# Three early blocks instead of two ahead of a mixture-of-experts pass, and a pass that begins with only its first kind of block made ready

## The chip, the cores and the metric

The kernel runs on one core of one Trainium2 chip. The metric is the device time of one launch in microseconds (us); before the change the median of three runs was 2474.57 us (2471.67 to 2475.16). A row of the profile names the engine: PE is TensorE's matmul and PEld its weight load, DVE is VectorE, ACT is ScalarE, POOL is GpSimd, SP is SyncE, which here only issues transfers. L1563 is line 1563 of the kernel before.

## The reference

The input is `x`, 64 graphs of 256 nodes with 256 features (16,384 tokens), and an integer adjacency matrix per graph. Two layers follow each other:

```
x = x + graph_attention(layernorm(x), adj)
x = x + mamba2(layernorm(x))
x = x + relational_conv(layernorm(x), adj)
x = x + moe_ffn(layernorm(x))          # 8 experts, the best one per token

# moe_ffn, for each token t:
idx  = argmax(softmax(t @ gate_w + gate_b))
y    = relu(t @ w1[idx] + b1[idx]) @ w2[idx] + b2[idx]    # 256 -> 1024 -> 256
y    = y * probability(idx)                               # zero beyond an expert's capacity
y    = nan_to_num(y)
```

An expert takes at most 2,560 tokens. Only the last line, the mixture of experts (MoE), and the point where the rest hands over to it, are touched by the change, apart from one small store at the very start.

## The kernel before

**Pass 1** does everything up to the choice of the expert. It goes through the tokens in 32 groups of 512 rows. Its instructions are not written in the order in which they run: each step is recorded with a duration, the tiles that it reads and writes, and a rank, and a planner (`Plan`, a list scheduler) lays them out once, at build time. The rank of a step of group g is `PACE * g` plus an entry of the table `DUE`; the steps that come behind all groups take theirs from the table `LATE`, in the order in which they are recorded. A tile has a name (a "home") with a fixed number of buffers; a step that needs a home is laid out after the steps that use its previous tenant. The program order on each engine's queue is what the planner gave; the engines wait for each other by semaphores.

Each group stores its rows into `x3d` in memory and, for every token, a slot of four numbers (token number, weight, mean, scale) into `slots`, which is sorted by expert. `out` already has the rows at that point; the MoE part overwrites them.

**Early blocks.** An expert's tokens are worked on in blocks of 512 slots. When 28 of the 32 groups are routed, `list_first` picks the first `NEARLY` blocks that are already full, and `first_block` records their whole computation with the planner, so that it can be laid between the last groups' steps. Such a block fetches its slots and the expert's weights (SP), gathers its 512 rows from `x3d` by four indirect DMAs of 128 rows (L409, POOL), normalises them (L415, DVE), turns them (L1367 on PE, with copies on ACT), multiplies by `w1` (the L744 row `ps<-eT,gate` or its twin for block 0; ReLU at L1379 on ACT), by `w2` (L1388), adds the bias (L1394), scales (L1396, ACT), replaces non-finite values (`guarded`, L420 to L424), adds the residual (L1402) and scatters four times 128 rows into `out` (L427, POOL). The block has no memory of its own: it lives in homes of pass 1. Block 0 has `xT`, `xn`, `xnT` and four buffers of `x`, block 1 has `adji`, `wh`, `eT` and three of `dm`; each has one of the two buffers of `gate` (for `w1`) and of `xh` (for `w2`).

`list_blocks` then lists the remaining work: full blocks of 512 ("wholes"), and of each expert's rest, at most one block of 256 ("halves") and blocks of 128 ("quarters").

**Pass 2** (`second_pass`) has three loops, quarters, halves, wholes, in this order; each is a nest of `tc.If`, one per block, so its trip count is known only at run time. The trace shows 4 quarters, 1 half and 18 wholes. Each kind has a class `Blocks` with three buffers for slots and rows and two for weights (quarters with odd numbers use the wholes' second weight buffers). The body, `experts(i)`, first fetches the weights of block i+1 (`fetch_weights`, L1511 to L1520: `w1`, `b1`, `w2`, `b2`, all on SP's queue) and the slots of block i+2 (`fetch_slots`, L1502), gathers the rows of block i+2, normalises block i+1, then does its own multiplication by `w1` (32 matmuls at L1563, ReLU at L1567), by `w2` (16 matmuls per 128 rows, L1573), turns block i+1 in the middle (`turned`: L1545 on PE, L1548 on ACT), and finishes its rows (L1578, L1579, L420 to L424, L1586, L427).

So whatever block 0 of a loop needs has to be made ready before the loop. The kernel before does this for all three kinds ahead of the first loop, step by step in the order of its code: six slot fetches (blocks 0 and 1 of each kind), six gathers (14 indirect DMAs, since a whole takes four, a half two and a quarter one), three weight fetches, three times normalise and turn. Then comes a test, `general` (L1612 to L1617: two DVE instructions, a tiny matmul and a copy), whose outcome decides after pass 2 whether the inputs need a second, general form of the kernel. Pass 2's tiles lie in the memory that pass 1's homes had; a write waits for the last use of the home under it.

**The very start.** Before pass 1, the weights are prepared. One result, `b1` in a transposed form, is written to memory (`b1d`, L591) from SP's queue; SP then issues the loads of the first groups (L805 for `adj`, L803 for `x`).

Of the kernel before, what the change touches and what calls it, by code (L numbers as in the profile page):

```python
# [9 lines left out]
F32 = mybir.dt.float32  # L10
# [4 lines left out]
ALU = mybir.AluOpType  # L15
AX = mybir.AxisListType
# [3 lines left out]
P = 128  # L20
# [39 lines left out]
    1921, 332, 270, 332, 389, 145, 449, 139, 514, 497, 334, 177, 408, 502, 1660, 1834, 1843, 1988,  # L60
    2202, 2247, 2273, 2186, 2179, 1985, 1853, 1933, 1944, 2220, 1882, 2133, 1815, 2009, 2179,
    2095, 1789, 1828, 563, 1802, 1733, -146, 109, 1792, 2073, 414, 1763, 1943, 143, 509, 2344,
    2010, 508, 2033, 2085, 250, 423, 2196, 2256, 716, 2018, 1585, 411, 176,
]


# [221 lines left out]
def gnn_mamba_rgcn_moe(ctx: ExitStack, tc: tile.TileContext, a: dict, out: bass.AP):  # L288
# [12 lines left out]
    nc = tc.nc  # L301
    x, adj = a["x"], a["adj"]
    B, N, D = x.shape
    assert N == 256 and D == 256 and B % 2 == 0
    T = B * N
    NG = B // 2
# [26 lines left out]
    b1d = dram.tile([E, P, NFT], F32, name="b1d")  # L333
# [6 lines left out]
    for blk in (0, 2):  # L340
        nc.gpsimd.affine_select(
            out=tri[:, blk, :], in_=tri[:, blk, :], compare_op=ALU.is_ge, fill=0.0,
# [3 lines left out]
    upper, ones_pp = tri[:, 0, :], tri[:, 1, :]  # L346
# [29 lines left out]
    work = const.tile([1, 3, 2, NBLK], I32, name="work")  # L376


    NEARLY = 2
    early = const.tile([1, 2, NEARLY], I32, name="early")  # L380
    taken = const.tile([P, E], F32, name="taken")
    num_i = const.tile([P, NBLK], I32, name="num_i")
# [5 lines left out]
    tested = const.tile([P, NG], F32, name="tested")  # L388
    general = const.tile([1, 1], I32, name="general")
# [42 lines left out]
    def first_pass(form, pass1):  # L432
# [28 lines left out]
        for q in range(2):  # L461
            nc.scalar.dma_start(
                out=dch[q * 64 : (q + 1) * 64, :], in_=dskip[q : q + 1, :].broadcast_to([64, NCT])
# [50 lines left out]
        with tc.tile_pool(name="prep" + form, bufs=1) as prep, tc.tile_pool(  # L514
            name="prep_ps" + form, bufs=2, space=PSUM
# [8 lines left out]
                out=gq0[:, :, 0:E], in_=a["L1_ffn_gate_w"].rearrange("(k p) e -> p k e", p=P)  # L524
# [10 lines left out]
            for vec, dst in (("L0_ffn_b_lin", blin), ("L1_gnn_bias", brel)):  # L535
                col = prep.tile([P, 2], F32, tag="col", name="col", bufs=2)
                nc.sync.dma_start(out=col, in_=a[vec].rearrange("(k p) -> p k", p=P))
                ps = prep_ps.tile([P, 512], F32, tag="ps0", name="ps")
                for k in range(2):
                    nc.tensor.matmul(  # L540
                        ps[:, : E + 1], lhsT=col[:, k : k + 1].to_broadcast([P, P]),
                        rhs=gq[:, k, : E + 1],
                        start=(k == 0), stop=(k == 1),
# [4 lines left out]
            for i in range(2):  # L548
                nc.sync.dma_start(
                    out=av[:, i, :],  # L550
                    in_=a["L0_gnn_a"][i * D : (i + 1) * D, :].rearrange("d o -> o d").broadcast_to([P, D]),
# [17 lines left out]
            for k in range(2):  # L569
                ps = prep_ps.tile([P, DI], F32, tag="ps0", name="ps")  # L570
# [5 lines left out]
            for c in range(NCT):  # L576
                ps = prep_ps.tile([P, DG], F32, tag="ps0", name="ps")
                for k in range(2):
                    nc.tensor.matmul(
                        ps, lhsT=woT[:, k, c * P : (c + 1) * P], rhs=wl[:, k, :],  # L580
                        start=(k == 0), stop=(k == 1),
# [5 lines left out]
            ps = prep_ps.tile([P, E * NFT], F32, tag="ps0", name="ps")  # L587
            nc.tensor.transpose(ps, b1r, ident[: E * NFT, : E * NFT])
            b1t = prep.tile([P, E, NFT], F32, name="b1t")
            nc.vector.tensor_copy(b1t.rearrange("p e k -> p (e k)"), ps)  # L590
            nc.sync.dma_start(out=b1d.rearrange("e p k -> p e k"), in_=b1t)  # L591


        xv = x.rearrange("b (h p) d -> p (b h) d", p=P)
# [24 lines left out]
        def counted(s, tot):  # L619

            ps, seen_ = s.psum(), s.fixed(seen)
            s.step(PE, 0.1, lambda: nc.tensor.matmul(
                ps()[:, :E], lhsT=tri_b[:, 1, :], rhs=seen, start=True, stop=True), [seen_], [ps])
            s.step(DVE, 0.08, lambda: nc.vector.tensor_copy(tot(), ps()[:, :E]), [ps], [tot])
# [5 lines left out]
        def walk(s, we, wb, past, n, ends, gap, limit, to):  # L630

            v = nc.vector
            s.step(DVE, 0.07, lambda: v.memset(we(), 0.0), [], [we])
            for e in range(E - 1):
                def passed(e=e):
                    v.tensor_scalar(past(), num[:, :n], ends()[:, e : e + 1], None, ALU.is_ge)
                    v.tensor_add(we(), we(), past())
                    v.scalar_tensor_tensor(wb(), past(), gap()[:, e : e + 1], wb(), ALU.mult, ALU.add)  # L640

                s.step(DVE, 0.4, passed, [ends, gap], [we, wb, past])

            def listed():
                v.tensor_scalar(wb(), wb(), float(limit - 1), None, ALU.min)
                v.tensor_copy(to[:, 0, :n], we()[0:1, :])
                v.tensor_copy(to[:, 1, :n], wb()[0:1, :])

            s.step(DVE, 0.25, listed, [we, wb], [s.fixed(to)])

        def list_first(s):
# [3 lines left out]
            tot, full, ends, gap = (s.tile(n + "_", [P, E]) for n in ("tot", "full", "ends", "gap"))  # L655
            we, wb, past = (s.tile(n + "_", [P, NEARLY]) for n in ("we", "wb", "past"))
            counted(s, tot)
# [14 lines left out]
            def took():  # L672
                v.tensor_scalar(tot(), ends(), float(NEARLY), None, ALU.min)
                v.tensor_copy(taken[:, 0:1], tot()[:, 0:1])
                v.tensor_sub(taken[:, 1:], tot()[:, 1:], tot()[:, : E - 1])
                v.tensor_scalar(gap(), full(), -1.0, float(NB), ALU.mult, ALU.add)
                v.tensor_copy(wb(), num[:, :NEARLY])

            s.step(DVE, 0.5, took, [ends, full], [tot, gap, wb, s.fixed(taken)])
            walk(s, we, wb, past, NEARLY, ends, gap, NBLK, early)  # L680

# [606 lines left out]
        def first_block(s, b, stored, source):  # L1288
# [5 lines left out]

            w1, w2 = s.tile("gate", [P, NCT, 512], bufs=2), s.tile("xh", [P, NCT, 512], bufs=2)
            side = s.tile("hide", [P, 4, N], BF16, bufs=3)
            if b == 0:
                xg, xn, xnT = s.tile("xT", [P, 2, 512]), s.tile("xn", [P, 4, D]), s.tile("xnT", [P, 2, 512])
                hid = [s.tile("x", [P, 4, DQ], bufs=5) for _ in range(4)]
            else:  # L1300
                xg, xn, xnT = s.tile("adji", [P, 4, N], I32), s.tile("wh", [P, 4, WX]), s.tile("eT", [P, 2, 512])
                hid = [s.tile("dm", [P, 2, 2, N + P], bufs=NCT) for _ in range(3)]
            each = NFT // len(hid) + (NFT % len(hid) > 0)

            def hidden(f):
                t = hid[f // each]()
                t = t.rearrange("p a b c -> p (a b c)") if b else t.rearrange("p a b -> p (a b)")
                return t[:, (f % each) * 512 : (f % each + 1) * 512]


# [51 lines left out]
            for k in range(2):  # L1362
                ps = s.psum()
# [10 lines left out]
            for f in range(NFT):  # L1374
                ps = s.psum()
# [6 lines left out]
            for j in range(4):  # L1382
                ps = s.psum()
# [39 lines left out]
        if form == "fast":  # L1423
# [15 lines left out]
            list_blocks(plan)  # L1439
            for b in range(NEARLY):  # L1440
                first_block(plan, b, rows_early, x3d[0 : GEARLY * 4 * P])
# [21 lines left out]
    def second_pass(form, pass2):  # L1463
        et = pass2.enter_context(tc.tile_pool(name="et" + form, reuse_waits="tile", bufs=2))
        es = pass2.enter_context(tc.tile_pool(name="es" + form, reuse_waits="tile", bufs=4))
        eps = pass2.enter_context(tc.tile_pool(name="eps" + form, reuse_waits="tile", bufs=8, space=PSUM))
# [124 lines left out]
        quarters = Blocks(2, wholes)  # L1591
# [6 lines left out]
        ]  # L1598
        three = (quarters, halves, wholes)
        for blocks in three:  # L1600
            for i in range(2):
                blocks.fetch_slots(i)
        for blocks in three:
            for i in range(2):
                blocks.gather(i, nc.gpsimd)
        for blocks in three:
            blocks.fetch_weights(0)
        for blocks in three:
            blocks.turned(blocks.norm(0), 0)
        if form == "fast":  # L1610
            other = es.tile([P, NG], F32, tag="yv", name="other")
            nc.vector.tensor_scalar(other, tested, float(N) + 1.0, None, ALU.is_gt)  # L1612
            others = es.tile([P, 1], F32, tag="others", name="others", bufs=1)
            nc.vector.tensor_reduce(others, other, AX.X, ALU.max)
            ps = eps.tile([P, 512], F32, tag="ps", name="ps")
            nc.tensor.matmul(ps[:, 0:1], lhsT=ones_pp, rhs=others, start=True, stop=True)
            nc.vector.tensor_copy(general, ps[0:1, 0:1])  # L1617
        for blocks in three:
            with ExitStack() as nest:  # L1619
                for i in range(blocks.most):  # L1620
                    nest.enter_context(tc.If(listed[blocks.kind] > i))
                    blocks.experts(i)


    for form in ("fast", "slow"):
        with ExitStack() as here:
            if form == "slow":
                again = nc.values_load(
                    general[0:1, 0:1], min_val=0, max_val=P,
                    skip_runtime_bounds_check_because="a count of partitions",  # L1630
                )
                here.enter_context(tc.If(again > 0))
            with ExitStack() as pass1:
                first_pass(form, pass1)
            with ExitStack() as pass2:
                second_pass(form, pass2)
# [34 lines left out]
```

## Time and profile before

The profile is of one execution, 37 us longer than the median of the runs.

| | us |
|---|---|
| median of the runs (lowest, highest) | 2474.57 (2471.67, 2475.16) |
| the profiled execution's own time | 2511.58 |
| its span, first to last instruction | 2509.9 |
| mean granted TensorE clock in it | 0.979 |
| PE busy (share of the span) | 2360.5 (94%) |
| DVE busy | 1917.8 (76%) |
| ACT busy | 1644.8 (66%) |
| POOL busy | 817.3 (33%) |

The page cuts the span into 40 slices of 62.7 us and gives each engine's busy share in each as a digit of tenths (9 is 90% or more), and the granted clock likewise. A row of the timeline has a start, a duration, the engine and line, the tiles (output, then inputs), the count of instructions run together, and in brackets the idle time before it with what ended it. A row of the windows view has, for a stretch of time, its length, each engine's busy time with a count, the granted clock, the busy share of the DMA engines and GB/s.

### The profile page before, as it was taken

The page shows a single profiled execution, that of the slowest core. Times are in us where ns is not written, and L with a number is a line of the kernel's source. Part 1 is how long each engine was busy: PE and PEld are TensorE (multiplying, and loading weights), DVE is VectorE, ACT ScalarE, POOL GpSimd, SP SyncE. Part 2 cuts the span into 40 slices and gives each one's busy share as a digit, 9 for nine tenths or more (in the row PEclk, how much of TensorE's full clock was granted, in tenths as well). Part 3 has the DMA queues.
Part 4 walks back from the last instruction along what each step waited for, and adds up shares of the span by engine and source line. Part 5 has one row for each costly group of instructions (what it writes and reads, how often), then busy time and mean ns, then how long its engine had stood idle before and what let it go on. Part 6 is the DMA issues. An engine that isn't in the chain of part 4 may idle for free.

```text
span 2509.9 us, 35018 instructions
## 1 busy us (share of the span) xinstructions
PE 2360.5 (94%) x11451; PEld 1645.5 (66%) x11451; DVE 1917.8 (76%) x4825; ACT 1644.8 (66%) x3720; POOL 817.3 (33%) x762
## 2 busy tenths in 40 slices
PE   5999999999999999999999999999986899999996
PEld 3667676767667666766766676676655666666664
DVE  4899899999989998998999999999863343344333
ACT  2878888878888887888888888887522233222331
POOL 1132424333342433334243333423423223222231
PEclk8999999999999999999999999999997999999998
DMA  3212222322222322222232222223337433333332
GB/s 115 44 23 62 54 71 65 71 54 54 62 54 71 68 68 54 54 62 54 70 71 65 54 54 62 57 59 55 105 96 244 135 128 112 124 108 112 124 113 65
DMA packets 173527, 198.93 MB, mean 79 GB/s; under 512 B 25448, under 2 KB 157870, under 8 KB 173312
## 3 DMA queue, kind: packets, MB, share of 16 engines
q1 hardware_dynamic: 124816, 135.70, 16.8%
q0 software_dynamic: 46816, 58.88, 12.8%
q8 instruction: 98, 1.61, 0.3%
q10 hardware_dynamic: 1680, 1.79, 0.3%
q14 instruction: 117, 0.96, 0.1%
HBM read 112.47 MB, written 45.45 MB: 63 GB/s over the span
## 4 chain that ended last, share of the span: by engine, by line
issue 31%; DVE 30%; PE 18%; POOL 10%; ACT 7%; DMA 3%; POOLq 0%; another core or an unknown queue 0%; SPq 0%; ACTq 0%; DVEq 0%
PE ps L744 12%; DVE y L963 8%; POOL xg L409 3%; POOL out_dram L427 3%; DVE gate L946 3%; POOL rs L752 3%; PE ps L1095 2%; DVE gate L1108 2%; DVE st L760 2%; DVE xh L1105 2%; DVE dm L1088 2%; DMA xg<-x3d,place 1%; DVE ev L857 1%; DVE bm L973 1%; DVE ev L859 1%
## 5 line engine op out<-in xcount | busy, mean ns | idle before, releaser
L744 PE MATMUL ps<-xnT,win 128*128 128x512 f32 x1152 | 544.5, 602 | 4.0 <-ACT xnT L786 4.0
L963 DVE SCALAR_TENSOR_TENSOR y<-ps,cw,y 128x510 f32<-128x510 f32 (+2 forms) x480 | 350.6, 737 | 6.5 <-ACT y L956 5.4
L1030 ACT ACTIVATE dm<-ps,cs 128x256 f32<-128x256 f32 (+1 forms) x1024 | 335.6, 480 | 24.2 <-PE ps L744 23.6
L752 POOL TENSOR_TENSOR rs<-ve,mhalf 128x4 f32<-128x4 f32 x96 | 149.0, 1552 | 570.3 <-DVE ve L750 447.6
L744 PEld LDWEIGHTS ps<-xnT,win 128*128 128x128 f32 x1152 | 205.4, 191 | 171.8 <-issue 156.9
L1563 PE MATMUL ps<-xnT,w 128*128 128x512 f32 (+2 forms) x736 | 277.1, 536 | 10.6 <-DVEq L1619 6.0
L1573 PE MATMUL ps<-w,hid 128*128 128x256 f32 x1248 | 276.3, 379 | 0.0
L1573 PEld LDWEIGHTS ps<-w,hid 128*128 128x128 f32 x1248 | 235.3, 190 | 38.7 <-issue 8.6
L744 PE MATMUL ps<-wf,gate 128*128 128x265 f32 x1024 | 251.9, 388 | 0.6 <-DVE gate L1108 0.6
L1088 DVE TENSOR_TENSOR dm<-dm,bc 128x1536 f32<-128x1536 f32 x128 | 225.9, 1766 | 2.8 <-ACT dm L1036 1.4
L1563 PEld LDWEIGHTS ps<-xnT,w 128*128 128x128 f32 x736 | 132.8, 195 | 144.6 <-issue 135.9
L744 PEld LDWEIGHTS ps<-wf,gate 128*128 128x128 f32 x1024 | 191.3, 190 | 48.6 <-issue 11.2
L1567 ACT ACTIVATE hid<-ps,b 128x512 f32<-128x512 f32 (+2 forms) x184 | 114.7, 624 | 162.8 <-PE ps L1563 153.0
L1578 DVE TENSOR_TENSOR yv<-ps,b 128x256 f32<-128x256 f32 x78 | 33.1, 425 | 224.8 <-PE ps L1573 224.7
L1095 PE MATMUL ps<-dm,xdt 128*64 128x256 f32 x1024 | 170.4, 399 | 32.8 <-DVE dm L1088 32.3
L1036 ACT ACTIVATE dm<-dm 128x1536 f32<-128x1536 f32 x128 | 199.2, 1559 | 0.0
L1282 POOL DMA_INDIRECT slots<-meta,sl x128 | 127.9, 1000 | 200.5 <-DVE sl L1279 149.3
L427 POOL DMA_INDIRECT out_dram<-yf,place x78 | 77.8, 997 | 310.9 <-DVE yf L1586 310.2
L760 DVE BATCH_NORM_STATS2 st<-x 128x6 f32<-128x256 f32 x384 | 151.3, 412 | 7.4 <-DMA x<-in_x_dram 6.8
L1579 ACT ACTIVATE yv<-yv,meta 128x256 f32<-128x256 f32 x78 | 39.9, 512 | 167.9 <-DVE yv L1578 167.9
L744 PE MATMUL ps<-wh,eT 128*128 128x273 f32 x512 | 142.4, 407 | 7.4 <-ACT eT L882 4.9
L969 ACT ACTIVATE xh<-y 128x512 f32<-128x512 f32 x160 | 101.2, 633 | 72.9 <-DVE y L963 64.3
(314 smaller groups left out, 5023.4 us busy)
## 6 DMA issues: line engine op xcount, KB each, us to landing
w<-in_L_ffn_w_dram SPq DMA_DIRECT2D x52, 1024.0 KB
x<-blin POOLq DMA_DIRECT2D x32, 530.0 KB
x<-brel POOLq DMA_DIRECT2D x32, 530.0 KB
adji<-in_adj_dram SPq DMA_DIRECT2D x32, 512.0 KB
x<-in_x_dram SPq DMA_DIRECT2D x32, 512.0 KB
x3d<-x SPq DMA_DIRECT2D x32, 512.0 KB
out_dram<-x SPq DMA_DIRECT2D x32, 512.0 KB
cm<-bm SPq DMA_DIRECT2D x32, 128.0 KB
```

What stands on the lines that cost most here:

```text
L427: apart("out", nc.gpsimd.indirect_dma_start(out=outf, out_offset=bass.IndirectOffsetOnAxis(ap=col, axis=0), in_=yf, in_offset=None, bounds ...
L744: nc.tensor.matmul(out_, lhsT=lhsT, rhs=rhs, start=(i == 0), stop=(i == len(pairs) - 1))
L752: s.step(POOL, 1.0, lambda: nc.gpsimd.tensor_tensor(rs(), ve(), mhalf[:, 0:4], ALU.pow), [ve], [rs])
L760: s.step(DVE, 0.34, lambda j=j: nc.vector.bn_stats(sb()[:, j, :], src()[:, j, 0:D]), [(src, j)], [(sb, j)])
L963: nc.vector.scalar_tensor_tensor(y3[:, :, d:], p3[:, :, : N - d], cw[:, c, k : k + 1], y3[:, :, d:], ALU.mult, ALU.add,)
L1030: nc.scalar.activation(dm()[:, q, bi, o : o + n], ps()[:, t0 + N - n : t0 + N], AF.Relu, bias=cs()[:, j, h : h + 1], scale=-1.0,)
L1036: s.step(ACT, 1.38, lambda: nc.scalar.activation(dm(), dm(), AF.Exp, scale=-1.0), [], [dm])
L1088: s.step(DVE, 1.67, lambda dm=dm: nc.vector.tensor_mul(dm(), dm(), bc().unsqueeze(1).to_broadcast([P, 2, 2, N + P])), [bc], [dm])
L1095: nc.tensor.matmul(o, lhsT=xdt()[:, 2 * bi, h * 64 : (h + 1) * 64], rhs=dm()[:, q, bi, 0:N], start=True, stop=False,)
L1282: s.step(POOL, 1.1, lambda j=j: apart("slots", nc.gpsimd.indirect_dma_start(out=slots, out_offset=bass.IndirectOffsetOnAxis(ap=sl()[:, j : ...
L1563: nc.tensor.matmul(ps[:, :n], lhsT=w1[:, k, f * P : (f + 1) * P], rhs=xnT[:, k, :], start=(k == 0), stop=(k == 1),)
L1573: nc.tensor.matmul(ps[:, :D], lhsT=hid[:, f, j * P : (j + 1) * P], rhs=w2[:, f, :], start=(f == 0), stop=(f == NFT - 1),)
```

## The change

1. `NEARLY` is 3. A third early block is recorded, with 48 more entries in `LATE` (a copy of the entries of the first block's steps). It takes the homes of block 0 (`b % 2 == 0`), and the third buffer of `hide` for its slots and biases.
2. The start of pass 2 is arranged anew. Slots of block 0 of each kind are fetched first; then, per kind, block 0 is gathered and the slots of block 1 fetched; then the weights of block 0 of each kind; only the quarters' block 0 is normalised and turned; block 1 of each kind is gathered; the quarters' loop begins. The halves' block 0 is normalised and turned behind the quarters' loop, followed by the test `general`; the wholes' block 0 behind the halves' loop.
3. The store of `b1d` goes from SP's queue to POOL's.

```
-    NEARLY = 2
+    NEARLY = 3

-            nc.sync.dma_start(out=b1d.rearrange("e p k -> p e k"), in_=b1t)
+            nc.gpsimd.dma_start(out=b1d.rearrange("e p k -> p e k"), in_=b1t)

-            if b == 0:
+            if b % 2 == 0:
                 xg, xn, xnT = s.tile("xT", [P, 2, 512]), s.tile("xn", [P, 4, D]), s.tile("xnT", [P, 2, 512])
                 hid = [s.tile("x", [P, 4, DQ], bufs=5) for _ in range(4)]
             else:

         for blocks in three:
-            for i in range(2):
-                blocks.fetch_slots(i)
+            blocks.fetch_slots(0)
         for blocks in three:
-            for i in range(2):
-                blocks.gather(i, nc.gpsimd)
+            blocks.gather(0, nc.gpsimd)
+            blocks.fetch_slots(1)
         for blocks in three:
             blocks.fetch_weights(0)
+        quarters.turned(quarters.norm(0), 0)
         for blocks in three:
-            blocks.turned(blocks.norm(0), 0)
-        if form == "fast":
...
-        for blocks in three:
+            blocks.gather(1, nc.gpsimd)
+        for k, blocks in enumerate(three):
             with ExitStack() as nest:
                 for i in range(blocks.most):
                     nest.enter_context(tc.If(listed[blocks.kind] > i))
                     blocks.experts(i)
+            if k < 2:
+                three[k + 1].turned(three[k + 1].norm(0), 0)
+            if k == 0 and form == "fast":
+                other = es.tile([P, NG], F32, tag="yv", name="other")
...
+                nc.vector.tensor_copy(general, ps[0:1, 0:1])
```

## The prediction

> **What bounds the kernel now.** I read the page's busy shares first, then the 40 slices, the timelines of the stretches that the change touches, their windows and transfers, and last SP's own waits. PE is busy for 94% of the span, so the change must be judged where PE is idle.
>
> ```profile
> PE   5999999999999999999999999999986899999996
> PEclk8999999999999999999999999999997999999998
> ```
>
> PE's digit falls below 9 at the start and in three slices around 1850 to 1980 us, the handover from pass 1 to pass 2. PE's timeline there:
>
> ```profile
> 47.89 1.94 PE L781 MATMUL ps<-ident,x 128*128 128x128 f32 x8 [7.48 <-DMA x<-in_x_dram]
> ...
> 1874.36 15.25 PE L1388 MATMUL ps<-xh,dm 128*128 128x256 f32 x62 [0.85 <-ACT dm L1379]
> 1904.12 0.69 PE L1545 MATMUL ps<-ident,xn 128*128 128x128 f32 x2 [14.51 <-DVE xn L415]
> ...
> 1917.98 5.73 PE L1563 MATMUL ps<-xnT,w 128*128 128x128 f32 x32 [0.16 <-issue]
> ...
> 1954.52 7.14 PE L1563 MATMUL ps<-xnT,w 128*128 128x256 f32 x32 [3.53 <-issue]
> ...
> 1975.02 15.18 PE L1563 MATMUL ps<-xnT,w 128*128 128x512 f32 x29 [6.01 <-DVEq L1619]
> ...
> 2006.01 13.90 PE L1563 MATMUL ps<-xnT,w 128*128 128x512 f32 x32
> ...
> 2034.43 13.90 PE L1563 MATMUL ps<-xnT,w 128*128 128x512 f32 x32
> ```
>
> The last early block leaves PE at 1874.36 + 15.25 = 1889.6; call this t0. The first quarter's multiplication starts 28.4 us later, and all that PE does in between is transposes as rows arrive. The quarters' loop ends at 1951.0 (t0 + 61.4), the half starts after 3.5 us of idle, the wholes after 6.0. From there each whole costs 2034.43 - 2006.01 = 28.42 us, seamless to the end. The windows view, for t0 to the first quarter, the half, and the wholes' first 6 us (columns: PE, PEld, DVE, ACT, POOL busy; clock; DMA share; GB/s):
>
> ```profile
> 1889.60:1918.00 28.40, 4.92 (x18) 2.53 (x17) 8.40 (x25) 2.51 (x7) 18.26 (x29) 0.59 0.70 219
> ...
> 1954.50:1969.00 14.50, 14.48 (x68) 12.46 (x68) 3.40 (x11) 4.85 (x11) 3.09 (x4) 1.00 0.71 201
> 1975.00:1981.00 6.00, 5.98 (x8) 2.55 (x9) 1.53 (x6) 0.69 (x1) 1.41 (x2) 0.58 0.02 5
> ```
>
> In the 28.4 us POOL is the busy engine. Its timeline: the last scatter of the early blocks, then 14 gathers, one every 1.3 us or so.
>
> ```profile
> 1895.67 0.97 POOL L427 DMA_INDIRECT out_dram<-y,hide  x1 [1.43 <-DVE other L1612]
> ...
> 1897.37 1.07 POOL L409 DMA_INDIRECT xg<-x3d,place  x1 [0.28 <-POOL place L406]
> ...
> 1915.81 0.96 POOL L409 DMA_INDIRECT xg<-x3d,place  x1 [0.30 <-issue]
> ```
>
> The first quarter's gather is issued at t0 + 7.8 and its rows are normalised at 1903.66, 6.3 later. Everything after waits for the wholes' rows, since they are normalised ahead of the loop (last at 1917.48).
>
> **The change, part by part.** Every term is a difference in the profiled execution (2511.58 us, span 2509.9); that one is 37 us above the median, 1.5%, which on terms of this size is under half a microsecond each, so the sum goes onto the median unchanged.
>
> *Start (`b1d` to POOL): -2.0.* SP's timeline:
>
> ```profile
> 40.90 0.39 SPq L591 DMA_DIRECT2D b1d<-b1t  x1
> 41.38 0.53 SPq L805 DMA_DIRECT2D adji<-in_adj_dram  x1
> 42.01 4.33 SPq L803 DMA_DIRECT2D x<-in_x_dram  x5
> ```
>
> PE waits for the first `x`. SP stands at L591 for 26.7 us (its chain of waits says so), with the first loads behind it. Without it, `adji` goes out during those 26.7 us and `x` once its home's last user (L583, 40.7) is done: 1.2 earlier, and half a megabyte of `adji` is no longer ahead of it (about 1.4 us at 0.36 MB/us, partly shared anyway). Bounds -0.7 to -2.9. POOL gets the store in front of clearing the slots, which nothing needs before the first routing.
>
> *Third block on PE: +30.0.* In the built order it stands wholly behind block 1's products. Its 8 transposes take 1.04 (the x8 row of a whole), the second copy 0.65, `w1` 8 x 1.72 = 13.7 (32 matmuls at 0.43), `w2` 64 x 0.22 = 14.1, plus 0.5 for seams; 29.5 to 32. Its weights wait for block 0's products (over by about 1862) and move at 1840 to 1870 under block 1; its gathers wait for block 0's last residual (L1402, about 1878.5), so its rows are normalised at about 1889, just when PE comes free. If that comes late, PE idles by as much. Behind that gather on POOL stand block 0's last scatter and block 1's; none of them is awaited by PE.
>
> *One whole fewer in pass 2: -28.4* (17 instead of 18).
>
> *From the third block's end, t0' = t0 + 30, to the quarters' end: -5.4.* POOL's order is as before: all scatters, then gathers, the first quarter's first. So its gather is issued at t0' + 7.8, normalised 6.3 later, multiplied 1.7 later: t0' + 15.8 instead of t0 + 28.4, 12.6 earlier, as only its own rows are waited for. But the weights come later. Before, two kinds' weights moved under block 1:
>
> ```profile
> 1868.24 4.66 SPq L1502 DMA_DIRECT2D meta<-slots  x6
> 1873.46 0.38 SPq L1511 DMA_DIRECT2D w<-in_L_ffn_w_dram  x1
> ...
> 1876.30 0.38 SPq L1511 DMA_DIRECT2D w<-in_L_ffn_w_dram  x1
> ...
> 1898.29 0.38 SPq L1511 DMA_DIRECT2D w<-in_L_ffn_w_dram  x1
> ...
> 1902.32 1.40 SPq L1511 DMA_DIRECT2D w<-in_L_ffn_w_dram  x1
> ```
>
> After, the slot fetches of pass 2 lie over homes of the third block: the first quarter's over its `w1`, the second quarter's over its `w2`. SP must wait for PE's last product of it, and all weight fetches queue behind. From about t0' + 5.2 there are to move: three sets of 2.23 MB (1.05 + 1.05 + 0.13), then the second quarter's `w1` (1.05), and 14 gathers of 0.131 MB: 9.6 MB. Before, 4.45 MB of weights and 0.56 MB of scatters moved in 1876 to 1889, 0.385 MB/us; with gathers mixed in, 6.24 MB in 1898 to 1920, 0.284, but not all that stretch had work queued. I take 0.36: the second quarter can start at about t0' + 32, though the first is done at 15.8 + 9.4 = 25.2. PE idles 6.5. Then 8 us each, with 0.7 for weights that arrive behind: 40, 48, 56. 56 - 61.4 = -5.4. Here a rule of the Trainium skill bears on it ("DMA: Bandwidth & Descriptors", section Where 436 GB/s comes from): one core gets some 358 GB/s from memory, while the fabric's ceiling is 435. The page's first figure gives my result; with the fabric's, the quarter's weights would be there at 27.3, the stall 2 and the term -10. The row decides: a peak over whole microseconds of 0.385. Bounds: no stall -12.6; at 0.284 the stall is 14 and the term +1.6.
>
> *Normalising and turning moved into the gaps between loops: +5.0.* Before the half: two L415 (0.8), four transposes in two pairs with a copy each, and the small test ahead of the loop, +2.0. Before the wholes: four L415 (1.6), eight transposes, two copies, +2.8; with semaphore hops 4.5 to 6. Nothing covers these: PE has nothing else queued.
>
> *Clock: +1.2.* The first whole lasts 2006.01 - 1975.02 = 30.99 instead of 28.42: after the 6.0 us gap the granted clock was 0.58 over 6 us, price 2.57. That is paid before and after. After the 3.5 us gap ahead of the half it was 1.00; this gap grows to 5.5. The skill ("TensorE: Matmul & The Clock Gate", Part 1: The HAM clock gate) halves the clock after an idle window of about 3.4 us that runs freely. Read strictly, both gaps would trip it and the half pay another 2.6; by the row, 3.5 tripped nothing, and 5.5 lies nearer to 6.0, which did. I take half of the price, 1.2 (0 to 2.6).
>
> Sum: -2.0 + 30.0 - 28.4 - 5.4 + 5.0 + 1.2 = **+0.4**, so 2475.0.
>
> **Rivals.** Within 0.2% (5 us) a measurement of this kernel tells nothing apart.
>
> *Slower: SP's burst.* The same stall, longer. All four sets queue behind t0', with gathers of 1 KB rows among them (2973 of the 3927 packets of 1898 to 1920 were under 2 KB), and at 0.284 MB/us the second quarter waits until t0' + 39: +7 on the sum, **2482**. It decides from about 9.6 / 31.4 = 0.306 MB/us downward (4.7 us later than I have it). For it: the stretch most like it ran at 0.284. Against: that stretch had 3 us of empty queue at its start, and 0.34 to 0.39 once it was full.
>
> *Faster: no stall.* The weights of the half and the whole, which are ahead of the second quarter's in SP's queue, go out early enough, because the slot waits end with `w1`'s last use, 14 us before t0', or because the queues share. The term is then nearly -12.6: **2467**. Against: the second quarter's slots are ahead of all weights in SP's order and lie over `w2`'s home.
>
> *Faster: the third block covers the empty stretch.* If the quarters' gathers could run under the third block's products, most of the 28.4 us would go: -2 + 30 - 28.4 - 27 + 6 = -22, **2453**. Against: POOL's order has the third block's scatters, which need its products, ahead of those gathers.
>
> *The change does not do what it says:* no third full block is there when the list is made. By then 28 of 32 groups are routed, and the trace has 18 wholes left after two early ones, so one is; I give this nothing.
>
> **From cases to numbers.** Forecast 0.44 (its own range 2470 to 2480), slower 0.33, no stall 0.15, cover 0.08. A range of 2466.5 to 2484.5 leaves out the cover and the outer tail of the burst (0.284 and a late third block, +9 and more). Faster by over 0.2%: cover and most of no stall, 0.22. Slower: 0.33. Same: 0.45.
>
> **What would show it.** L781's first row at about 46. The third block's L1388 rows ending 30 us after block 1's; if they start with idle time, the +30 is wrong. SP's slot fetches waiting for PE. The first quarter's L1563 at t0' + 15.8, the second's with 6 us of idle ended by a transfer of `w`: if there is no idle, "no stall" holds; if 12 or more, the burst. Gaps of 5.5 and 8.8 ahead of the half and the wholes, ended by ACT's copy. The clock in the half. 17 rows of 28.42. What would make me wrong most is the third block's start: a gather or a weight that comes late there is paid in full.

## The result

| | us |
|---|---|
| before, median of 8 runs (lowest, highest) | 2471.26 (2468.21, 2477.88) |
| after, median of 8 runs | 2480.23 (2479.73, 2482.71) |
| ratio, with its 95% interval | 1.0036 (1.0027 to 1.0045) |
| profiled execution of after: time, span, clock | 2481.96, 2480.1, 0.979 |

The change costs 0.36%, 9 us. That lies in the range given (2466.5 to 2484.5), but 9 us is more than the 5 us within which the forecast called it unchanged: it fell into the case "slower", to which 0.33 had been given, and, as will be seen, mostly not by the mechanism described there.

The two profiles can't be compared from start to end: the execution of before that was profiled for the prediction ran pass 1 some 40 us slower than that of after, spread over the groups (its last group begins at 1648.7 instead of 1607.9), and the times of the runs, 9 us apart the other way, show nothing of it. So the stretches are compared from marks inside the program. PE's timeline of after (start, duration, engine and line, tiles, count; idle before and what ended it), from the last group to the second whole (a line of after is four higher than the same line of before):

```profile
1785.35 0.58 PE L748 MATMUL ps<-adjT,xhi 128*128 128x256 f32 x1 [9.14 <-ACT xhi L800]
...
1839.62 14.39 PE L1392 MATMUL ps<-xh,dm 128*128 128x256 f32 x60
1853.85 1.04 PE L1371 MATMUL ps<-ident,xn 128*128 128x128 f32 x8
1855.13 14.00 PE L748 MATMUL ps<-xnT,gate 128*128 128x512 f32 x32 [0.24 <-ACT xnT L1376]
1868.97 13.98 PE L1392 MATMUL ps<-xh,x 128*128 128x256 f32 x64
1898.96 0.69 PE L1549 MATMUL ps<-ident,xn 128*128 128x128 f32 x2 [16.02 <-DVE xn L419]
1899.81 5.65 PE L1567 MATMUL ps<-xnT,w 128*128 128x128 f32 x32 [0.16 <-ACT xnT L1552]
...
1918.12 6.67 PE L1567 MATMUL ps<-xnT,w 128*128 128x128 f32 x32 [8.99 <-DMA w<-in_L_ffn_w_dram]
...
1949.83 9.62 PE L1567 MATMUL ps<-xnT,w 128*128 128x256 f32 x32
...
1971.13 1.79 PE L1549 MATMUL ps<-ident,xn 128*128 128x128 f32 x8 [4.34 <-DVE xn L419]
1973.17 15.05 PE L1567 MATMUL ps<-xnT,w 128*128 128x512 f32 x32 [0.25 <-ACT xnT L1552]
...
2002.75 13.90 PE L1567 MATMUL ps<-xnT,w 128*128 128x512 f32 x32
```

Much of it is as the working had it. The third block follows the second without a gap and takes 1882.95 - 1854.01 = 28.9 us. The first quarter starts 16.9 us after it, and ahead of the second one PE is idle for 9 us with a weight transfer as its releaser. The first line is what the working did not have: 9 us of idle in the last group of pass 1, long before the third block.

### The profile page after: what moved, and what is told of

Read it like the earlier page. It is cut to its first block, busy times and chain, and to the rows that moved or that the text cites. A ratio compares the mean times of both kernels' runs of the same rounds, so it can differ in the third digit from the quotient of the medians.

```text
span 2480.1 us, 35001 instructions
## 1 busy us (share of the span) xinstructions
PE 2357.6 (95%) x11448; PEld 1648.5 (66%) x11451; DVE 1914.2 (77%) x4825; ACT 1635.3 (66%) x3720; POOL 827.9 (33%) x763
## 5 line engine op out<-in xcount | busy, mean ns | idle before, releaser
L756 POOL TENSOR_TENSOR rs<-ve,mhalf 128x4 f32<-128x4 f32 x96 | 161.3, 1680 | 520.6 <-DVE ve L754 397.3
L1567 PE MATMUL ps<-xnT,w 128*128 128x512 f32 (+2 forms) x704 | 267.0, 541 | 10.0 <-DMA w<-in_L_ffn_w_dram 9.0
L1577 PE MATMUL ps<-w,hid 128*128 128x256 f32 x1184 | 262.1, 379 | 0.0
L1577 PEld LDWEIGHTS ps<-w,hid 128*128 128x128 f32 x1184 | 223.3, 190 | 36.7 <-issue 8.1
L1571 ACT ACTIVATE hid<-ps,b 128x512 f32<-128x512 f32 (+2 forms) x176 | 109.0, 619 | 159.3 <-PE ps L1567 157.9
```

The costliest lines, as they stand in the source:

```text
L756: s.step(POOL, 1.0, lambda: nc.gpsimd.tensor_tensor(rs(), ve(), mhalf[:, 0:4], ALU.pow), [ve], [rs])
L1567: nc.tensor.matmul(ps[:, :n], lhsT=w1[:, k, f * P : (f + 1) * P], rhs=xnT[:, k, :], start=(k == 0), stop=(k == 1),)
L1577: nc.tensor.matmul(ps[:, :D], lhsT=hid[:, f, j * P : (j + 1) * P], rhs=w2[:, f, :], start=(f == 0), stop=(f == NFT - 1),)
```

## Experiments

The first four ran on a chip on which the kernel before takes 2533.8 us, the next four on a second chip (2470.6), the last four on a third (2470.6 and 2471.1). Each ratio is against runs of the kernel before on the same chip; where two kernels ran on different chips, their distances from that kernel are compared. In what follows t0 is the end of the second early block on PE, and t0' that of the third.

**The kernel before, once more.** No edit.

> The kernel before, unchanged, profiled a second time, since its first profiled execution was 37 us above its median and pass 1 took 35 us less in the profile of the changed kernel. If that first one was an odd execution, pass 1 (first L781 to the last early block's last L1388) takes some 1806 us here as in the changed kernel, and the groups come at one pace. If the kernel before has a slower pass 1 of its own, it takes about 1842 us again. From the last early block's end to the end of the span: 620 us either way.

Measured: on this chip pass 1 is slow as well (the last group begins at 1666.2), so it decides nothing about the odd first profile. But it showed something else. From t0 to the end it took 623.3 us instead of 620.3, and 2.8 of the 3 us are in one row, the half's:

```profile
1974.99 9.95 PE L1563 MATMUL ps<-xnT,w 128*128 128x256 f32 x32 [3.54 <-issue]
```

In the first profile this row took 7.14 us after the same gap of 3.5. The window over it has a granted clock of 0.71 here and 1.00 there.

**b1d's store back on SP.**

```
-            nc.gpsimd.dma_start(out=b1d.rearrange("e p k -> p e k"), in_=b1t)
+            nc.sync.dma_start(out=b1d.rearrange("e p k -> p e k"), in_=b1t)
```

> The changed kernel with the store of b1d back on SP's queue. If the prediction's first term holds (-2.0), this is 2 us slower than the changed kernel, +11 against before. If the store on POOL only lets adj collide with the loads of the preparation and the first groups' x (the first group began 0.8 earlier, the second one 1.1 later), this is about 1 us faster than the changed kernel, +8 against before.

Measured: 1.0049 (1.0035 to 1.0063). The interval holds the first expectation (+11 us, 1.0043) and also the changed kernel's own 1.0036; the second one (+8, 1.0032) lies just below it. This leans towards a store that is worth something on POOL, but it decides nothing alone: the changed kernel itself did not run on this chip.

**Two early blocks, with the new start of pass 2.**

```
-    NEARLY = 3
+    NEARLY = 2
```

> The changed kernel with NEARLY = 2: only the new start of pass 2 and b1d. My theory: the third block's homes are what delays pass 2's weights. Here the first quarter's and the half's weights move under block 1 again, the first quarter starts 15 to 17 us after the last early block instead of 28.4, the second one follows without a stall or with one below 3 us, and the gaps ahead of half and wholes cost about +5 as in the changed kernel (2.0 and 0.5 of gap, 2.5 of clock): 5 to 8 us faster than before, 14 to 17 faster than the changed kernel. Rival: the stall comes from the order of the new start itself (the whole's weights and all gathers ahead of the second quarter's weights); then the second quarter waits about 9 us here too, and the time is within 3 us of before.

Measured: 0.9978 (0.9970 to 0.9986), 2528.55 against 2533.8, which is 5.2 us faster than before. The first quarter starts at t0 + 15.4, the second at t0 + 29.2 after 2.9 us of idle in between, no stall of 9. So the new start of pass 2, with the store on POOL, is a gain, and the third block loses it.

**The second quarter's weights ahead of the half's and the whole's.**

```
         for blocks in three:
             blocks.fetch_weights(0)
+            if blocks is quarters:
+                blocks.fetch_weights(1)
...
-                self.fetch_weights(i + 1)
+                if i or self.kind < 2:
+                    self.fetch_weights(i + 1)
```

> The changed kernel with the second quarter's weights fetched directly behind the first one's, ahead of the half's and the whole's. If the stall of 9 us is a matter of order in SP's queue, it goes, and the time falls by 6 to 9 us to that of before (0 to +3). Rival: the half's or the whole's weights are late in its place, the stall moves to the half (its weights then come behind four sets), and less than 4 us are won.

Measured: 1.0040 (1.0026 to 1.0053): nothing won. The rival was right in that, though the wait did not go to the half. The second quarter now begins to multiply at t0' + 31 instead of 35, but with stalls in the first one's products and in its own (2.2 and 2.7 us), and the third starts at t0' + 45.4, against 45.8 in the changed kernel. In the second of these stalls DVE stands 13.4 us until the third quarter's slots land, whose fetch is again behind the weights. The order in the queue only moves the wait to another place; the sum of what has to move stays.

**The changed kernel again**, as a reference on the second chip.

> The changed kernel itself, for comparison on the same chip with the runs beside it. As measured before: 1.0036 times the kernel before, about +9 us. In its profile: some 9 us of PE idle in the last group ahead of the L748 row with xhi, 9 us ahead of the second quarter.

Measured: 1.0030 (1.0020 to 1.0041), 2478.64 against 2470.58. The idle ahead of `xhi` is 8.98 us, that of the second quarter 8.49. SP's waits around t0' have this line for the slots of pass 2, behind which all weights stand (L1392 is the third block's `w2` product; wait in all, times, longest):

```profile
SPq L1506 <- PE ps L1392: 11.4, 1, 11.4
```

**The third block's places later on DVE.** In the changed kernel DVE has two instructions of the third block between the last group's statistics and its residuals, and in the trace they wait for the block's slots. This moves them behind the residuals:

```
-            s.step(SP, 3.5, fetch_slots, [listed_], [(side, "meta")], late=0.5)
+            s.step(SP, 3.5, fetch_slots, [listed_], [(side, "meta")], late=12.0 if b == 2 else 0.5)
```

> The changed kernel, but the planner is told that the third block's slots land 12 us after their fetch instead of 0.5, so that DVE's two instructions that turn them into places stand nine instructions later in its queue, behind the last group's residuals; nothing else moves. If DVE's wait for that fetch is what keeps PE idle for 9 us in the last group (2.5 before), the idle falls back to about 2.5 and the kernel is 6 to 7 us faster than the changed one, +2 to +3 against before. Rival: DVE's wait is only in front of another one (POOL or the rows being slow), PE stays idle there, and less than 2 us are won.

Measured: 1.0030 (1.0018 to 1.0041), no change, and PE is idle for 8.94 us at the same place. The theory that DVE's wait is the cause falls. POOL's timeline in this run shows what was behind it:

```profile
1765.70 1.42 POOL L795 DMA_DIRECT2D x<-brel  x1 [0.23 <-DVE pos L1281]
1779.43 1.10 POOL L1286 DMA_INDIRECT slots<-meta,sl  x1 [12.31 <-DMA hide<-slots]
1780.83 1.00 POOL L1286 DMA_INDIRECT slots<-meta,sl  x1 [0.30 <-issue]
1781.84 1.08 POOL L756 TENSOR_TENSOR rs<-ve,mhalf 128x4 f32<-128x4 f32 x1
```

POOL stands for 12.3 us ahead of a scatter of routing results into the `slots` memory, until the third block's fetch out of the same memory has landed. The power that the last group's normalisation needs (L756) is behind it in POOL's queue; ACT's `xhi` waits for that, and PE for `xhi`. In the changed kernel's own trace the same wait had DVE's place as its releaser, since both were released by the same landing. ACT's timeline there (second chip), then SP's, which has what was ahead of the fetch:

```profile
1783.64 1.70 ACT L800 ACTIVATE xhi<-x,rs 128x256 fp32r<-128x256 f32 x4 [14.46 <-POOL rs L756]
```

```profile
1766.51 0.37 SPq L1350 DMA_DIRECT2D gate<-in_L_ffn_w_dram  x1
...
1767.66 0.37 SPq L1353 DMA_DIRECT2D xh<-in_L_ffn_w_dram  x1
...
1769.59 0.34 SPq L1340 DMA_DIRECT2D hide<-slots  x1
```

Two megabytes of the second block's weights were issued 3.1 and 1.9 us ahead of the 16 numbers per partition that POOL waits for; the second of these megabytes takes 11.1 us from issue to landing, the 8 KB behind it 9.6. That the fetch lands late because of them is read from the queue: no run puts the fetch ahead of the weights, and half a megabyte from POOL's own queue (`x<-brel`) moved in the same time.

**b1d alone.** The kernel before with only the store moved to POOL.

> The kernel before with b1d's store on POOL and nothing else. My prediction's term was -2.0. The profiles with it show the first group 0.8 to 1.1 earlier and the second one 0.2 to 1.4 later than without; by the second group, from which all goes on, it is worth between -1 and +1: no difference that can be measured, 0.9995 to 1.0005.

Measured: 0.9998 (0.9990 to 1.0007), no difference that could be seen; the interval reaches from -2.5 to +1.7 us. Since pass 1 and pass 2 are otherwise those of before, and its profile has no odd pass 1, this profile stands for "before" in the account below. At the place where PE stands 9 us in the changed kernel, the scatter and PE wait this long in it:

```profile
1768.78 1.10 POOL L1282 DMA_INDIRECT slots<-meta,sl  x1 [0.44 <-DVE sl L1279]
```

```profile
1778.98 0.39 PE L744 MATMUL ps<-adjT,xlo 128*128 128x256 f32 x1 [2.69 <-DVE xlo L1172]
```

**The third block alone.** Pass 2's start and `b1d` as before; the third block with its entries in `LATE`, of which the change adds 59, not 48.

> The changed kernel with pass 2's start and b1d as before: the third block alone. By the numbers of the changed kernel's profile: 29.0 for the block, 28.4 less for a whole, 6.5 for DVE's wait in the last group, and the first quarter 28.4 after the third block as before; its weights have to come from t0' + 5 on, of which about 8.4 of 9.6 MB are through by then, so the second quarter waits 3 to 4: together +10 to +11 against before, 1.004. Rival: if the new start of pass 2 costs time of its own, this is faster than the changed kernel.

Measured: 1.0050 (1.0036 to 1.0064), 12.4 us slower. The idle ahead of `xhi` is 8.94 here too, so it comes with the third block. The rival does not hold: without the new start of pass 2 the kernel is slower, not faster. The wait of 3 to 4 us that was expected ahead of the second quarter is not there (0.25 us): with the first quarter at t0' + 29.7 the weights had come. So the 12.4 us are not in all their parts those of the expectation.

**The third block's slots fetched behind the lists.** Now the fetch itself is moved out of the way, instead of one of those that wait for it. The lists are ready after the last slot scatter, so nothing is left that could wait for the fetch.

```
-            s.step(SP, 3.5, fetch_slots, [listed_], [(side, "meta")], late=0.5)
+            s.step(SP, 3.5, fetch_slots, [listed_] + [s.fixed(lists[2])] * (b == 2), [(side, "meta")], late=0.5)
```

> The changed kernel with the third block's slots fetched behind the last groups' slot scatters (it waits for the last of the lists). My theory after the run that only moved DVE's two instructions: what waits is POOL. Its scatters into the slots memory must not overtake the third block's fetch from it, that fetch lands 10 us after its issue because 2 MB of the second block's weights are ahead of it, and the power that PE needs stands behind the scatter in POOL's queue. Then the idle of 9 us ahead of the L748 row with xhi falls back to about 2.5 and the time falls by 6 to 7 us, to +1 to +2 against before. Rival: the last group's rows are late for another reason; no change, 1.003.

Measured: 0.9998 (0.9990 to 1.0007), 2471.23 against 2470.63: of the 8.1 us by which the changed kernel was slower, 0.6 are left. In its trace the scatter and the power go through at once, and the idle in the last group is back to 2.5. POOL's timeline, then PE's:

```profile
1769.36 1.10 POOL L1286 DMA_INDIRECT slots<-meta,sl  x1 [0.44 <-DVE sl L1283]
1770.76 1.00 POOL L1286 DMA_INDIRECT slots<-meta,sl  x1 [0.30 <-issue]
1771.76 1.08 POOL L756 TENSOR_TENSOR rs<-ve,mhalf 128x4 f32<-128x4 f32 x1
```

```profile
1779.37 0.39 PE L748 MATMUL ps<-adjT,xlo 128*128 128x256 f32 x1 [2.49 <-DVE xlo L1176]
```

The fetch goes out at 1823.5 here instead of 1769.6, and the third block loses nothing by it: it still follows the second one with 0.2 us between.

**The half's and the whole's weights later.** Fewer bytes ahead of the second quarter.

```
-        for blocks in three:
-            blocks.fetch_weights(0)
+        quarters.fetch_weights(0)
...
+            if k == 0:
+                halves.fetch_weights(0), wholes.fetch_weights(0)
```

> The changed kernel with the half's and the whole's weights fetched behind the quarters' loop. If the stall ahead of the second quarter is the sum of bytes that must move from t0' on (9.6 MB), and not the third block's homes as such, 4.46 MB fewer are ahead of it: its weights are there at about t0' + 19, before the first quarter ends at 25, the idle of 8.5 goes, and the quarters' loop ends 7 to 8 us earlier. The half's weights then come during the last two quarters. Time 7 to 9 us below the changed kernel, 1.000. Rival, as in the run with the second quarter's weights first: the third and fourth quarter wait in its place and less than 3 us are won.

Measured: 1.0009 (1.0001 to 1.0018), 2473.24 against 2470.63: 2.6 us above before instead of 8.1, so 5 to 6 us won where 7 to 9 were expected. The stall is gone (the second quarter follows the first with 0.3 us between), and the fourth quarter starts at t0' + 42.7 instead of 52.6. That the stall is set by the bytes ahead of the second quarter's in the queue is shown: with fewer it goes, in another order it does not. But the wholes start only 3.5 us earlier, at 84.6 instead of 88.1, since 6 us come back ahead of them:

```profile
1966.70 2.11 PE L1549 MATMUL ps<-ident,xn 128*128 128x128 f32 x8 [10.73 <-DVE xn L419]
```

DVE is late there because inside the half's body it first stands 18.1 us, until 1959.1. What stands there in its queue needs the slots of the next half but one, whose fetch SP issues only at 1953.3, behind the weights that were moved. No run has both mends, the third block's slots later and these weights later, so whether a third block can be made to pay stays open.

**Two versions built on the finding.** Both have two early blocks and the new start of pass 2. In the first one the first quarter's slots, gather, normalisation and transposes are recorded with the planner under the second block (new tiles of their own, 3 KB per partition), the second quarter's weights are fetched ahead of the half's, and the whole's behind the quarters' loop:

```
             for b in range(NEARLY):
                 first_block(plan, b, rows_early, x3d[0 : GEARLY * 4 * P])
+            first_rows(plan, rows_early)
...
+            s.step(SP, 3.5, fetched, [s.fixed(lists[2])], [meta], late=1.0)
+            s.step(DVE, 0.16, lambda: placed(place(), meta()), [meta], [place])
+            s.step(POOL, 1.1, lambda: gathered(xg()[:, 0, :], place()[:, 1, 0:1], x3d),
+                   [place, stored], [xg], late=9.0)
...
```

> Two early blocks and the new start of pass 2, with the first quarter's slots, gather, norm and turn recorded with the planner ahead of the second block's end, its weights and then the second quarter's fetched first, the half's next and the whole's behind the quarters' loop. By the profile with two early blocks, PE idles 15.4 us between the second block and the first quarter for POOL's gather chain, and 3 us in the first quarter. If that chain is all that is in the way, the first quarter starts within 1 us of the second block's end and the time falls by 12 to 16 us against that kernel: 18 to 21 us below before, 0.992. Rival: the first quarter starts early and then the second one waits for its own gather or weights, and half of it is lost: 0.995.

Measured: 0.9977 (0.9967 to 0.9987), no better than two early blocks alone. The first quarter starts with the end of the second block, 15 us earlier, and then the second one is 8.9 us idle for its rows, the third 6.1, and the whole 9.8: the rival's course, only that all of the gain is lost and not half of it. In the second version the second quarter's rows are planned too, all four sets of weights go ahead of the loop, and POOL keeps its order as written, with the whole's gathers behind the quarters' loop:

```
+        with tc.manual_schedule(engines={mybir.EngineType.Pool}):
...
+            for i in range(2):
+                halves.gather(i, nc.gpsimd)
+            quarters.fetch_weights(0)
+            quarters.fetch_weights(1)
+            halves.fetch_weights(0)
+            wholes.fetch_weights(0)
...
+                if k == 0:
+                    wholes.gather(0, nc.gpsimd)
+                    wholes.gather(1, nc.gpsimd)
```

> As the run with the first quarter planned, with the second quarter's slots and rows planned as well, all four first sets of weights ahead of the loop in the order first quarter, second quarter, half, whole, and the whole's eight gathers behind the quarters' loop in POOL's queue. In that run the first quarter started with the second block's end, and what it won was lost to the second quarter's rows (8.9 us of idle), the third's (6.1) and the whole's (9.8). If POOL's queue of gathers was what they waited for, the quarters now follow each other with less than 3 us of idle in all and the time falls by 12 to 20 us against before, 0.992 to 0.995. Rival: it is the weights, since the rate is the same; the third quarter waits for them, and it stays at 0.997.

Measured: 0.9954 (0.9940 to 0.9967), 2458.45 against 2471.07: 12.6 us faster than before, where the changed kernel is 8 to 9 slower. That is the lower edge of the 12 to 20 that were expected, and the condition named with it was not met: PE is idle for 11.8 us inside the second quarter, not for less than 3 in all. PE's timeline:

```profile
1842.61 3.62 PE L1402 MATMUL ps<-xh,dm 128*128 128x256 f32 x16
1846.07 3.73 PE L1617 MATMUL ps<-q_turned,w 128*128 128x128 f32 x32
...
1868.43 2.07 PE L1617 MATMUL ps<-xnT,w 128*128 128x128 f32 x8 [11.76 <-DVE yv L1632]
...
1875.57 3.84 PE L1617 MATMUL ps<-q_turned,w 128*128 128x128 f32 x32 [0.30 <-ACT q_turned L1601]
```

The 11.8 us that are left are again DVE in a loop's body. DVE's timeline shows which instruction it stands at:

```profile
1852.10 0.41 DVE L429 TENSOR_SCALAR xn<-r_rows,r_meta 128x256 f32<-128x256 f32 x1 [0.39 <-DVE y L1416]
1867.83 0.15 DVE L419 CAST place<-meta 128x1 int32<-128x1 f32 x1 [15.32 <-DMA meta<-slots]
```

It waits 15.3 us for the third quarter's slots, which are fetched behind the weights, and the second quarter's results wait behind it.

## Why the prediction was right or wrong

The range held, but by luck: its upper part was there for a longer stall ahead of the second quarter, and another wait took it up. The change was forecast at +0.4 us and measured at +9.0 at first and +8.1 on the second chip; what the sum covered was nearly right, and it left out a term of 7. The account, from the changed kernel's second profile against the profile with b1d alone (both on the second chip; differences in us):

| step of the prediction | predicted | measured | from |
|---|---|---|---|
| start, b1d | -2.0 | 0 (-2.5 to +1.7) | the run with b1d alone; the two profiles both have the store on POOL (last group at 1607.4 and 1608.0) |
| (not in the sum) last group to t0 | 0 | +7.3 | 245.9 against 238.6 |
| third block on PE | +30.0 | +28.9 | t0' - t0 |
| one whole fewer | -28.4 | -28.4 | rows of 28.42 |
| to the quarters' end | -5.4 | -1.6 | t0' + 60.2 against t0 + 61.7 |
| gaps between the loops | +5.0 | +2.5 | half 5.5 against 3.7, wholes 6.5 against 5.9 |
| clock in the half and the first whole | +1.2 | -2.1 | half 15.9 against 17.0, first whole 30.7 against 31.6 |
| sum | +0.4 | +6.6 | spans: +5.6; medians of the runs with the same two kernels: +7.6 |

- **The step that failed is "third block on PE".** It costed the block's weights as hidden and put the scatters behind its gathers at nothing, since PE awaits none of them. The block's slots fetch, which the change puts between the last slot scatters, is in no term. These scatters wait for the fetch, and the power (L756) ahead of PE's relational product stands behind them in POOL's queue. PE's idle there grew from 2.7 to 9.0 us, shown by the run that moves the fetch alone. The two megabytes of weights behind which the fetch stands were at that place of SP's queue in the profile of before as well (issued at 1809.9 and 1811.0). My first theory, DVE's two instructions, was a reading of the releaser column alone, and a run refuted it.
- **Start.** The run with b1d alone shows no gain, but its interval does not exclude the -2.0. In the profiles the first part of the step is there: PE's wait ahead of the first `x` is 6.8 to 7.5 us with the store on SP and 4.5 with it on POOL. But SP then waits 5.4 to 6.5 us within the loads of `x` for the store to land, so the five loads, issued from 42.9 on, spread over 8.9 us instead of 4.3. The second group begins 34.2 to 35.1 us after the start of the preparation's last product without the change and 33.5 to 34.1 with it in eight of ten profiles (32.7 and 31.7 in the others), so about 1 us is left. The step took the first arrival for the whole.
- **Second quarter.** The mechanism was right: SP stands until the third block's last product, and the bytes behind it set the time. The transfers of after moved 10.85 MB at a mean of 350 GB/s in the 31 us from 1887 to 1918; I had taken 360. The stall was 8.5 and 9.0 us in the two profiles of the changed kernel instead of 6.5, and the idle gave the second quarter a cold clock (5.4 to 6.7 us instead of 3.84), which the step left out. Of the two figures of the Trainium skill ("DMA: Bandwidth & Descriptors", Where 436 GB/s comes from) this mean is near that of the memory, 358. But 358 is no ceiling here: single slices of 0.8 us ran at up to 412, and the prediction's own row, 0.385 MB/us over 13 us, already lay above it. So that row did not decide for the page's first figure, and that 0.36 came out nearly right is in part luck.
- **Rival "burst".** It set its deciding point at a stall longer by 4.7; it was longer by 2 to 2.5. It did not decide; the case came true by another wait.
- **The other rivals.** The stall was there, so "no stall" falls. PE is idle for 15.5 to 16 us between the third block and the first quarter, so nothing was covered; the run that plans the first quarter's gather ahead shows that this idle can be had, and that the next waits then take it back unless they are moved as well.
- **Gaps.** Ahead of the half +1.9, as worked out. Ahead of the wholes +0.6 instead of +2.8: PE is idle for 4.3 us there and then has 1.9 us of transposes, where before it was idle for 5.9 throughout. DVE finishes the half's last rows in the first 3.1 us of it, and the four normalisations, which begin 3.8 us into it, run mostly beside the transposes. The step had added all of that to the gap of before.
- **Clock.** I took the row (a gap of 3.5 left the clock at 1.00) for half an argument against the rule of the Trainium skill ("TensorE: Matmul & The Clock Gate", Part 1: The HAM clock gate), by which an idle window of 3.4 trips it. In two of three profiles with the old loops the gap of 3.5 to 3.7 did trip it: the half's first product took 9.95 and 9.69 instead of 7.14. The price that I put on the change is mostly paid before as well. One row of one execution was not enough to weigh against a rule about a window that runs freely; nor does the rule alone foretell two of three, since a whole window of 3.4 would seldom lie within a gap of 3.5. No run here settles that.

What the sum did cover came out at -0.7 instead of +0.4, by errors that cancel; and without the slots' wait the changed kernel measures 0.9998. The account's own noise is some 3 us: the profiled execution with b1d alone is 3.2 us above the median of its runs, that of the changed kernel 1.2.

## What to carry to other kernels

Cost every transfer that a change adds, the smallest first: a fetch of 8 KB, put behind 2 MB in a queue and in front of a scatter into the same memory, cost 7 us, and it was not needed until some 50 us later, while 29 us of added products were paid back by the block removed elsewhere. When a small instruction is the releaser of a wait, ask what it was itself waiting for, and test by moving that. And work taken from a loop and put under another stage takes its transfers' window with it: here the third block filled PE, but it lay on the memory for the next stage's first slots, and all its weights stand behind those in the queue.

## What the runs showed of the hardware

- A gap of 3.5 us ahead of the same products tripped the clock in two of three executions and not in the third (granted clock 0.71, 0.73 and 1.00).
- With weights and gathers of 1 KB rows mixed, 350 GB/s were sustained over 31 us (the changed kernel, from 1887 to 1918).
- A fetch of 8 KB, issued 3.1 and 1.9 us behind two transfers of 1 MB in the same queue, landed 9.6 us after its issue (the changed kernel, second chip).
- The kernel before differs by 63 us, 2.6%, between two chips (2470.6 and 2533.8). Of the profiles on them, pass 1 differs by 58 us (its last group begins at 1608.0 in the one with b1d alone, at 1666.2 in that of the kernel before); why is open.
